# The second layer's mixture of experts: a run-time branch for each expert, and the output bias by a one-row matmul

## The chip, the core and the metric

The kernel runs on one core of one Trainium2 chip, as one launch. The metric is the device time of that core in microseconds. All data are 32-bit floats. The activations stay on the chip from the first load to the last store: `x_sb`, 128 partitions by 32 tiles of 128 columns, 4096 tokens of 128 features in all.

## The reference, cut to what matters

Six residual steps follow each other on `x` of shape (4, 1024, 128): mixture 0, a selective scan, mixture 0 again, mixture 1, attention over 16 heads and 16 "wavelengths", mixture 1 again. The change touches mixture 1 alone, which is run twice, before and after the attention:

```python
def _L1_ffn_ref(tokens, gate_w, w1, b1, w2, b2):
    ...
    cap = int(CAPACITY_FACTOR * N / E)
    x = tokens.reshape(N, H)
    probs = jax.nn.softmax(x @ gate_w.T, axis=-1)
    top2_w, top2_idx = jax.lax.top_k(probs, 2)
    ...
    counts = jnp.bincount(a_e, length=E)
    keep = counts <= cap
    valid = keep[a_e]
    ...
    h = jax.nn.silu(jnp.einsum('ech,efh->ecf', buf, w1) + b1[:, None, :])
    y = jnp.einsum('ecf,egf->ecg', h, w2) + b2[:, None, :]
    contrib = y[a_e, p] * (a_w * valid.astype(x.dtype))[:, None]
    out = contrib.reshape(N, 2, H).sum(axis=1)
    ...
x = x + 0.5 * _L1_ffn_ref(_layernorm(x, axis=-1), ...)
```

N is 4096 tokens, E is 8 experts, every token goes to its two best ones. The capacity is int(1.25 x 4096 / 8) = 640. An expert that more than 640 tokens chose is dropped as a whole: all of its contributions count as zero.

## The kernel before, in words

Everything is written with a tile framework that orders the instructions of each engine by itself and sets the semaphores. `STAGES` (line 1003) lists the stages; each group of stages loads its weights first, by DMAs on SyncE's queue (line 952), into memory that the group before has released.

`moe1` (line 388) is mixture 1. Its first half, the routing, loops over four groups of 1024 tokens. For each it takes the layer norm and transposes it into `xnt` (lines 73 to 112), forms the gate's logits on TensorE (`lg`, line 120), and ranks the experts of every token on VectorE (lines 121 to 141). This leaves `w`: for every token and expert, half the softmax weight where the expert is one of the best two, and zero elsewhere. Then the counts are summed over the tokens, across partitions by a matmul with ones (`pc`, line 416), compared with the capacity (`keep`, line 418), and `w` is multiplied by the result (line 419). So a dropped expert has weight zero for every token.

The second half computes densely: every expert runs on all tokens, whatever its weights. It loops over eight blocks of 512 tokens. In a block comes first the output bias for all experts at once: the four tiles of `w` are transposed (line 429), copied to SBUF by ScalarE (line 431), multiplied with the 8 x 128 matrix of biases (line 434) and added to `x_sb` (line 435). Then, for each of the eight experts, one unit of work: one matmul of 512 columns into `hp` (line 440), SiLU with bias on ScalarE (line 442), four matmuls of 128 columns into `op` (line 445), and four VectorE instructions that add `op` times the token's weight to `x_sb` (line 449). A matmul of 32-bit floats is two instructions with two weight loads. A call of `moe1` has 64 such units, 128 in the two calls. `hp` and `op` have three PSUM buffers each, `h` four in SBUF.

After the first call comes `attention`. It loads its own weights, works out two small tables, and has the kernel's only run-time branch: a flag is loaded into a register of every engine (line 574) and `tc.If` (line 580) chooses between two bodies. In this run the first body is executed and the second, long one is jumped over at the end. Inside, ScalarE takes 1024 exponentials of 128 x 8192 elements (line 804). After the second call of `moe1` the four quarters of `x_sb` are stored by DMAs (line 1029), each when its eight tiles are final.

Of the kernel before, what the change touches and what calls it, by code (L numbers as in the profile page):

```python
# [19 lines left out]
F32 = mybir.dt.float32  # L20
I32 = mybir.dt.int32
AF = mybir.ActivationFunctionType
ALU = mybir.AluOpType
AX = mybir.AxisListType
PSUM = bass.MemoryType.PSUM

P = 128
B, L, C = 4, 1024, 128
GT = L // P
NT = B * GT  # L30
E = 8
FS = 2
CAP = int(1.25 * B * L / E)
# [59 lines left out]
def layernorm_t(nc, k, sb, ps, g, out):  # L93

    x_g = k.x_sb[:, ts(g, GT), :]
    mv = sb.tile([P, GT, 2], F32, name="ln_mv")
    rstd = sb.tile([P, GT], F32, name="ln_rstd")
    ln_stats(nc, sb, x_g, mv, rstd)
    for i0 in range(0, GT, 4):
        pt = ps.tile([P, 4, P], F32, name="pt", tag="tr")  # L100
        for i in range(i0, i0 + 4):
            xn = sb.tile([P, C], F32, name="ln_xn", bufs=4)
            nc.vector.tensor_scalar(
                xn,
                x_g[:, i, :],
                mv[:, i, 0:1],
                rstd[:, i : i + 1],
                op0=ALU.subtract,
                op1=ALU.mult,
            )  # L110
            nc.tensor.transpose(pt[:, i - i0, :], xn, k.ident)  # L111
        nc.scalar.copy(out[:, i0 * P : (i0 + 4) * P], pt.rearrange("p a b -> p (a b)"))


def route(nc, k, sb, ps, xnt, w_router, ex, mask):


    lg = ps.tile([P, GT, E], F32, name="lg", tag="tr")
    for i in range(GT):
        nc.tensor.matmul(lg[:, i, :], xnt[:, ts(i, P)], w_router, start=True, stop=True)  # L120
    mx = sb.tile([P, GT], F32, name="rt_mx")
    nc.vector.tensor_reduce(mx, lg, AX.X, ALU.max)  # L122
    d = sb.tile([P, GT, E], F32, name="rt_d")
    nc.vector.tensor_tensor(d, lg, mx[:, :, None].to_broadcast([P, GT, E]), op=ALU.subtract)
    nc.scalar.activation(ex, d, AF.Exp)

    key = sb.tile([P, GT, E], F32, name="rt_key")
    nc.vector.tensor_scalar(key, d, LN_TINY, None, op0=ALU.max)
    other = key[:, :, None, :].to_broadcast([P, GT, E, E])
    own = key[:, :, :, None].to_broadcast([P, GT, E, E])  # L130
    eq = sb.tile([P, GT, E, E], F32, name="rt_eq")
    nc.vector.tensor_tensor(eq, other, own, op=ALU.is_equal)  # L132
    nc.vector.tensor_tensor(  # L133
        eq, eq, k.tri[:, None, :, :].to_broadcast([P, GT, E, E]), op=ALU.mult
    )
    above = sb.tile([P, GT, E, E], F32, name="rt_above")
    nc.vector.tensor_tensor(above, other, own, op=ALU.is_gt)  # L137
    nc.vector.tensor_tensor(above, above, eq, op=ALU.add)  # L138
    rank = sb.tile([P, GT, E], F32, name="rt_rank")
    nc.vector.tensor_reduce(rank, above, AX.X, ALU.add)  # L140
    nc.vector.tensor_scalar(mask, rank, 2.0, None, op0=ALU.is_lt)
# [245 lines left out]
def moe1(tc, k):  # L387


    nc = tc.nc  # L390
    with (
        tc.tile_pool(name="m1_all", bufs=1) as al,
        tc.tile_pool(name="m1", bufs=2) as sb,
        tc.tile_pool(name="m1_tr", bufs=2, space=PSUM) as ps_tr,
        tc.tile_pool(name="m1_h", bufs=3, space=PSUM) as ps_h,
        tc.tile_pool(name="m1_o", bufs=3, space=PSUM) as ps_o,
    ):
        xnt = al.tile([P, B, L], F32, name="xnt")
        mask = al.tile([P, NT, E], F32, name="mask")
        w = al.tile([P, NT, E], F32, name="w")  # L400
        for g in range(B):
            layernorm_t(nc, k, sb, ps_tr, g, xnt[:, g, :])
            ex = sb.tile([P, GT, E], F32, name="ex")
            gt = ts(g, GT)
            route(nc, k, sb, ps_tr, xnt[:, g, :], k.wr1, ex, mask[:, gt, :])
            tot = sb.tile([P, GT], F32, name="tot")
            nc.vector.tensor_reduce(tot, ex, AX.X, ALU.add)
            nc.vector.reciprocal(tot, tot)
            nc.vector.scalar_tensor_tensor(
                ex, ex, 0.5, tot[:, :, None].to_broadcast([P, GT, E]), op0=ALU.mult, op1=ALU.mult  # L410
            )
            nc.vector.tensor_tensor(w[:, gt, :], ex, mask[:, gt, :], op=ALU.mult)
        cnt = al.tile([P, E], F32, name="cnt")
        nc.vector.tensor_reduce(cnt, mask.rearrange("p t e -> p e t"), AX.X, ALU.add)
        pc = ps_tr.tile([P, E], F32, name="pc", tag="tr")
        nc.tensor.matmul(pc, k.ones, cnt, start=True, stop=True)  # L416
        keep = al.tile([P, E], F32, name="keep")
        nc.vector.tensor_scalar(keep, pc, float(CAP), None, op0=ALU.is_le)
        nc.vector.tensor_tensor(
            w, w, keep[:, None, :].to_broadcast([P, NT, E]), op=ALU.mult  # L420
        )

        for blk in range(NT // 4):
            t0 = blk * 4
            g, cols = blk // 2, ts(blk % 2, 512)

            pw = ps_tr.tile([E, 4, P], F32, name="pw", tag="tr")
            for i in range(4):
                nc.tensor.transpose(pw[:, i, :], w[:, t0 + i, :], k.ident)  # L429
            wt = sb.tile([E, 4, P], F32, name="wt")  # L430
            nc.scalar.copy(wt, pw)
            op = ps_o.tile([P, 4, C], F32, name="op")
            for i in range(4):
                nc.tensor.matmul(op[:, i, :], wt[:, i, :], k.b2_1, start=True, stop=True)  # L434
            nc.vector.tensor_tensor(
                k.x_sb[:, t0 : t0 + 4, :], k.x_sb[:, t0 : t0 + 4, :], op, op=ALU.add
            )
            for e in range(E):
                hp = ps_h.tile([P, 512], F32, name="hp")
                nc.tensor.matmul(hp, k.w1_1[:, e, :], xnt[:, g, cols], start=True, stop=True)  # L440
                h = sb.tile([P, 512], F32, name="h", bufs=4)
                nc.scalar.activation(h, hp, AF.Silu, bias=k.b1_1[:, e : e + 1])  # L442
                op = ps_o.tile([P, 4, C], F32, name="op")
                for i in range(4):
                    nc.tensor.matmul(  # L445
                        op[:, i, :], h[:, ts(i, P)], k.w2_1[:, e, :], start=True, stop=True
                    )
                for i in range(4):
                    nc.vector.scalar_tensor_tensor(  # L449
                        k.x_sb[:, t0 + i, :],  # L450
                        op[:, i, :],
                        w[:, t0 + i, e : e + 1],
                        k.x_sb[:, t0 + i, :],
                        op0=ALU.mult,
                        op1=ALU.add,
                    )

# [489 lines left out]
def getter(nc, pool, k):  # L949
    def get(name, shape, src, eng=nc.sync):  # L950
        t = pool.tile(shape, F32, name=f"c_{name}", tag=f"c_{name}")
        eng.dma_start(out=t, in_=src)
        setattr(k, name, t)

    return get
# [20 lines left out]
def load1(nc, pool, k, a):  # L976

    get = getter(nc, pool, k)
    get("wr1", [C, E], a["L1_ffn_gate_w"])
    get("w1_1", [C, E, P], a["L1_ffn_w1"])  # L980
    get("b1_1", [P, E], a["L1_ffn_b1"])
    get("w2_1", [P, E, C], a["L1_ffn_w2"])
    get("b2_1", [E, C], a["L1_ffn_b2"])


def load_attention(nc, pool, k, a):
# [16 lines left out]
STAGES = (  # L1003
    (load0, (moe0, s6, moe0)),
    (load1, (moe1,)),
    (load_attention, (attention,)),
    (load1, (moe1,)),
)

# [86 lines left out]
```

## Time and profile before

| | |
|---|---|
| median of 3 runs | 8990.91 us (8985.83 to 9001.39) |
| the profiled execution | 8990.01 us, of which the span is 8988.1 us |
| busy in it: PE, ACT, DVE, POOL | 8025.7, 7765.2, 3401.7, 609.2 us |
| granted TensorE clock, mean | 0.926 of full speed |
| instructions on TensorE | 77802 matmuls, 77802 weight loads |
| DMA, whole span | 19.43 MB, of which 10.01 MB on q8 are instructions |

How to read the lines further on. Times are microseconds unless marked ns. PE is TensorE's matmul, PEld its weight load; DVE is VectorE, ACT is ScalarE, POOL is GpSimd, SP is SyncE. A name with a q at its end (PEldq, DVEq, SPq) is the engine's sequencer, which executes waits, register loads, branches and DMA issues; these are not counted as busy. "x" is a number of instructions. A group's line ends with busy time, the mean ns of one, then the idle time of the engine just before it and who ended that. In a timeline the columns are start, length, engine, line, operation, and in brackets the idle time before. "issue" as a releaser means that the engine waited for nothing that the profile shows.

### The profile page before, as it was taken

How to read it: one execution, taken by the hardware profiler on the slowest of the kernel's cores; microseconds unless marked ns; L12 is line 12 of the kernel's file. 1: busy time of each engine (PE TensorE's matmuls, PEld its weight loads, DVE VectorE, ACT ScalarE, POOL GpSimd, SP SyncE). 2: the span in 40 equal slices, each digit the busy share in tenths (PEclk: the TensorE clock that was granted, in tenths of full speed). 3: DMA queues.
4: the chain of work that ended last, by engine and by line, in shares of the span. 5: the costliest groups of instructions: out<-in, count | busy, mean ns of one | idle time of the engine just before them, and what ended most of it. 6: DMA issues, size and time to landing. Idle time of an engine off the chain costs nothing. (4 is left out here: it accounts for less than half of the span.)

```text
span 8988.1 us, 167582 instructions
## 1 busy us (share of the span) xinstructions
PE 8025.7 (89%) x77802; PEld 3526.4 (39%) x77802; DVE 3401.7 (38%) x5903; ACT 7765.2 (86%) x1891; POOL 609.2 (7%) x579
## 2 busy tenths in 40 slices
PE   8888888899999998999999999898999998989877
PEld 5222265333333333333333333333333333333335
DVE  6776765333333333333233323333333233333225
ACT  3333333999999999999999999999999999999993
POOL 3444530000000000000000000000000000000000
PEclk9777798999999999999999999999999999999998
DMA  0000000000000000000000000000000000000000
GB/s 18 0 0 0 0 6 3 1 1 1 1 1 1 1 1 1 1 1 1 1 1 1 1 1 1 1 1 1 1 1 1 1 1 1 1 1 1 1 1 15
DMA packets 14355, 19.43 MB, mean 2 GB/s; under 512 B 3000, under 2 KB 12752, under 8 KB 13648
## 3 DMA queue, kind: packets, MB, share of 16 engines
q8 instruction: 611, 10.01, 0.5%
q1 hardware_dynamic: 9344, 6.01, 0.2%
q10 hardware_dynamic: 4304, 2.62, 0.1%
q14 instruction: 96, 0.79, 0.0%
HBM read 6.53 MB, written 2.10 MB: 1 GB/s over the span
## 5 line engine op out<-in xcount | busy, mean ns | idle before, releaser
L804 ACT ACTIVATE p_w<-xs,cc 128x8192 f32<-128x8192 f32 x1024 | 7187.6, 7109 | 37.8 <-DVE xs L742 26.8
L813 PE MATMUL o<-p_w,vt 128*9 128x256 f32 x65536 | 4051.5, 403 | 647.7 <-ACT p_w L804 645.5
L813 PEld LDWEIGHTS o<-p_w,vt 128*9 128x9 f32 x65536 | 1798.9, 95 | 2607.7 <-ACT p_w L804 799.9
L821 DVE COPY os<-o 128x256 f32<-128x256 f32 x1024 | 434.8, 425 | 3583.2 <-PE o L813 3583.0
L704 PE MATMUL s<-kp,qp 32*128 32x512 f32 x2048 | 1023.1, 619 | 0.0
L704 PE MATMUL s<-qp,kp 32*128 32x512 f32 x2048 | 1021.6, 618 | 0.0
L742 DVE COPY xs<-s 128x1024 f32<-128x1024 f32 x512 | 627.1, 1225 | 730.5 <-PE s L704 716.1
L718 DVE TENSOR_REDUCE nm<-s 128x1 f32<-128x1024 f32 x512 | 626.4, 1223 | 644.6 <-PE s L704 644.6
L704 PEld LDWEIGHTS s<-qp,kp 32*128 32x128 f32 x2048 | 343.1, 185 | 491.6 <-issue 487.4
L704 PEld LDWEIGHTS s<-kp,qp 32*128 32x128 f32 x2048 | 343.2, 186 | 470.7 <-issue 465.4
L834 PEld LDWEIGHTS pt<-ident,os 128*128 128x128 f32 x2048 | 205.7, 141 | 763.6 <-issue 667.6
L354 PE MATMUL yp<-hm,ident 128*128 128x512 f32 x512 | 382.8, 867 | 104.9 <-POOL hm L353 103.0
L834 PE MATMUL pt<-ident,os 128*128 128x128 f32 x2048 | 448.7, 301 | 20.0 <-DVE os L821 9.6
L336 ACT ACTIVATE da<-delta,neg_a 128x512 f32<-128x512 f32 x256 | 182.7, 721 | 299.0 <-DVE hst L342 298.5
L353 POOL TENSOR_TENSOR hm<-hst,c_sb 128x512 f32<-128x512 f32 x256 | 370.2, 1459 | 168.9 <-ACT c_sb L333 115.3
L178 ACT ACTIVATE r<-hp 128x512 f32<-128x512 f32 x160 | 95.6, 597 | 206.6 <-PE hp L176 185.7
L354 PEld LDWEIGHTS yp<-hm,ident 128*128 128x128 f32 x512 | 108.1, 248 | 349.7 <-POOL hm L353 317.5
L340 DVE TENSOR_TENSOR db<-du,bp 128x512 f32<-128x512 f32 x256 | 164.1, 681 | 162.9 <-PE bp L329 162.0
L442 ACT ACTIVATE h<-hp,c_b 128x512 f32<-128x512 f32 x128 | 87.6, 687 | 154.0 <-PE hp L440 153.9
L333 ACT COPY c_sb<-cp 128x512 f32<-128x512 f32 x128 | 74.9, 585 | 161.1 <-PE cp L331 126.3
L342 DVE TENSOR_TENSOR_SCAN hst<-da,last,db 128x512 f32<-128x512 f32 x128 | 190.6, 1528 | 0.0
L180 POOL TENSOR_TENSOR h<-r 128x512 f32<-128x512 f32 x160 | 164.8, 1048 | 200.7 <-ACT r L178 200.2
(180 smaller groups left out, 3820.1 us busy)
## 6 DMA issues: line engine op xcount, KB each, us to landing
x_sb<-in_L_attn_x_dram ACTq DMA_DIRECT2D x4, 512.0 KB
c_w<-in_L_ffn_w_dram SPq DMA_DIRECT2D x4, 512.0 KB
out_dram<-x_sb SPq DMA_DIRECT2D x4, 512.0 KB
c_w<-in_L_ffn_w_stack_dram SPq DMA_DIRECT2D x1, 512.0 KB
c_w<-in_L_ffn_w_stack_dram ACTq DMA_DIRECT2D x1, 512.0 KB
c_ws<-in_L_ffn_ws_dram SPq DMA_DIRECT2D x2, 128.0 KB
c_w_in<-in_L_attn_W_in_dram SPq DMA_DIRECT2D x1, 256.0 KB
c_w_out<-in_L_attn_W_out_dram SPq DMA_DIRECT2D x1, 128.0 KB
```

What stands on the lines that cost most here:

```text
L180: nc.gpsimd.tensor_tensor(h, r, r, op=ALU.mult)
L336: nc.scalar.activation(da, delta[:, c, hc], AF.Exp, scale=neg_a[:, c, n : n + 1])
L342: nc.vector.tensor_tensor_scan(hst, da, db, 0.0 if half == 0 else last[:, c, n : n + 1], op0=ALU.mult, op1=ALU.add,)
L353: nc.gpsimd.tensor_tensor(hm, hst, c_sb, op=ALU.mult)
L354: nc.tensor.matmul(yp[c], k.ident, hm, start=(n == 0), stop=(n == NS - 1))
L704: nc.tensor.matmul(s[:, ts(half, 512)], a[row, ts(i, P)], c[row, ts(half, 512)], start=True, stop=True,)
L718: nc.vector.tensor_reduce(nm[:, i : i + 1], score(j, qp[n], i, kp[n]), AX.X, ALU.max, negate=True)
L742: nc.vector.tensor_copy(xs[u][:, i, :], score(j, kp[n], i, qp[n]))
L804: nc.scalar.activation(p_w.rearrange("p a b -> p (a b)"), xs[u].rearrange("p a b -> p (a b)"), AF.Exp, scale=cc[:, h, wl : wl + 1],)
L813: nc.tensor.matmul(o[32 * r : 32 * r + D + 1, 0:QW], vts[b % 2][:, i, h, :], p_w[:, i, ts(r, QW)], start=(i == 0), stop=(i == GT - 1),)
L821: nc.vector.tensor_copy(os, o[:, 0:QW])
L834: nc.tensor.transpose(pt[:, wl % 2 * 2 + c, :], os[:, ts(c, P)], k.ident)
```

## The change

`moe1` alone is changed, and how one of its inputs is loaded.

- `keep` becomes an integer tile, and `w` is no longer multiplied by it. Two new VectorE instructions follow: `least`, the smallest of the eight counts, and `some`, whether that one is within the capacity.
- The loop over blocks and experts is turned inside out: `expert(e)` runs one expert over all eight blocks. It stands in `tc.If` on `keep[e]`, and the eight of these stand in an outer `tc.If` on `some`. `truth` loads one value into a register of every engine.
- The bias of all experts at once (transposes, copy, matmul, addition) is gone. In its place every one of the four `op` matmuls of a unit is followed by one that accumulates onto the same PSUM area: a row of ones times the expert's row of `b2`. The bias matrix is loaded as one row on one partition instead of eight rows.

```diff
-        keep = al.tile([P, E], F32, name="keep")
+        keep = al.tile([P, E], I32, name="keep")
         nc.vector.tensor_scalar(keep, pc, float(CAP), None, op0=ALU.is_le)
-        nc.vector.tensor_tensor(
-            w, w, keep[:, None, :].to_broadcast([P, NT, E]), op=ALU.mult
-        )
-
-        for blk in range(NT // 4):
-            t0 = blk * 4
-            g, cols = blk // 2, ts(blk % 2, 512)
-
-            pw = ps_tr.tile([E, 4, P], F32, name="pw", tag="tr")
-            for i in range(4):
-                nc.tensor.transpose(pw[:, i, :], w[:, t0 + i, :], k.ident)
-            wt = sb.tile([E, 4, P], F32, name="wt")
-            nc.scalar.copy(wt, pw)
-            op = ps_o.tile([P, 4, C], F32, name="op")
-            for i in range(4):
-                nc.tensor.matmul(op[:, i, :], wt[:, i, :], k.b2_1, start=True, stop=True)
-            nc.vector.tensor_tensor(
-                k.x_sb[:, t0 : t0 + 4, :], k.x_sb[:, t0 : t0 + 4, :], op, op=ALU.add
-            )
-            for e in range(E):
+        some = al.tile([P, 1], I32, name="some")
+        least = al.tile([P, 1], F32, name="least")
+        nc.vector.tensor_reduce(least, pc, AX.X, ALU.min)
+        nc.vector.tensor_scalar(some, least, float(CAP), None, op0=ALU.is_le)
+
+        def truth(tile_, j):
+            return nc.values_load(
+                tile_[0:1, j : j + 1],
+                min_val=0,
+                max_val=1,
+                skip_runtime_bounds_check_because="a comparison's result is 0 or 1",
+            )
+
+        def expert(e):
+
+            for blk in range(NT // 4):
+                t0 = blk * 4
+                g, cols = blk // 2, ts(blk % 2, 512)
                 hp = ps_h.tile([P, 512], F32, name="hp")
                 nc.tensor.matmul(hp, k.w1_1[:, e, :], xnt[:, g, cols], start=True, stop=True)
                 h = sb.tile([P, 512], F32, name="h", bufs=4)
...
                 for i in range(4):
                     nc.tensor.matmul(
-                        op[:, i, :], h[:, ts(i, P)], k.w2_1[:, e, :], start=True, stop=True
+                        op[:, i, :], h[:, ts(i, P)], k.w2_1[:, e, :], start=True, stop=False
+                    )
+                    nc.tensor.matmul(
+                        op[:, i, :], k.ones[0:1, :], k.b2_1[:, e, :], start=False, stop=True
                     )
...
+        with tc.If(truth(some, 0) > 0):
+            for e in range(E):
+                with tc.If(truth(keep, e) > 0):
+                    expert(e)
...
-    get("b2_1", [E, C], a["L1_ffn_b2"])
+    get("b2_1", [1, E, C], a["L1_ffn_b2"].rearrange("(o e) c -> o e c", o=1))
```

## The prediction, made before the changed kernel was run

> **What bounds the kernel now.** I read the busy slices of the page first, then the busy time of each engine in stretches cut at the stage borders, then single stretches by groups and in order of time.
>
> ```profile
> core 0: us, PE busy (x) PEld busy (x) DVE busy (x) ACT busy (x) POOL busy (x), PEclk, DMA share, GB/s
> 1285.20:1335.30 50.10, 29.14 (x112) 21.46 (x112) 38.14 (x194) 13.28 (x20) 0.00 (x0) 0.64 0.07 22
> 1335.30:1467.20 131.90, 129.11 (x722) 90.33 (x722) 75.54 (x266) 46.43 (x69) 0.00 (x0) 0.97 0.00 1
> 1545.80:8769.30 7223.50, 6541.14 (x72817) 2787.33 (x72816) 2226.36 (x3188) 7185.60 (x1025) 0.00 (x0) 0.95 0.01 1
> 8851.40:8983.60 132.20, 129.37 (x722) 90.42 (x722) 75.65 (x266) 46.43 (x69) 0.00 (x0) 0.97 0.05 13
> ```
>
> The third row is the attention: ACT is busy 7185.6 of 7223.5 us, so it sets 80% of the span, and the change doesn't touch it. Rows two and four are the dense halves of the two calls of moe1: 131.9 and 132.2 us, PE busy in 98% of each. Nothing of another stage runs beside them: the next stage's weights (first call) and the last store (second call) wait for their end. So whatever leaves these 264 us leaves the span. The first row is the first call's routing.
>
> What one unit of expert work costs PE, in the first call's tail:
>
> ```profile
> 1451.73 1.88 PE L440 MATMUL hp<-xnt,c_w 128*128 128x512 f32 x4
> 1453.59 2.05 PE L445 MATMUL op<-c_w,h 128*128 128x128 f32 x16
> 1455.48 1.88 PE L440 MATMUL hp<-xnt,c_w 128*128 128x512 f32 x4
> ```
>
> Two units return after 3.75 us: 1.88 us a unit at full clock, PE without gaps.
>
> **Which experts run.** The profile can't say, the weights are data. Evaluating the reference's routing on its own inputs gives, for the first call, the counts 938, 1180, 733, 853, 1478, 886, 949, 1175: all over 640, so `some` is false and everything is jumped over. For the second: 960, 1100, 798, 1345, 1107, 1539, 587, 756: expert 6 alone is kept. Nearest to the limit are 587 and 733, far enough that rounding doesn't decide.
>
> **What a branch costs.** The one branch of the kernel shows it: the sequencers' rows of the flag's load and of the comparison, then VectorE at the attention's end, where the second body is jumped over.
>
> ```profile
> L574 SPq TENSOR_LOAD <-flag x1: 466/466/466, 1472.4 to 1472.4; - x1
> L574 PEldq TENSOR_LOAD <-flag x1: 492/492/492, 1472.5 to 1472.5; - x1
> L574 DVEq TENSOR_LOAD <-flag x1: 544/544/544, 1476.9 to 1476.9; - x1
> ...
> L580 PEldq COMPARE_BRANCH  x2: 92/1920/3747, 1473.0 to 8795.0; - x2
> L580 DVEq COMPARE_BRANCH  x2: 51/53/55, 1477.5 to 8796.2; - x2
> ```
>
> ```profile
> 8796.19 0.29 DVE L510 TENSOR_TENSOR x_sb<-x_sb,c_bo 128x128 f32<-128x128 f32 x1
> 8799.11 0.49 DVE L78 BATCH_NORM_STATS2 ln_st<-x_sb 128x6 f32<-128x128 f32 x2 [2.63 <-issue]
> ```
>
> A branch that falls through costs PE 0.49 (load) + 0.09 + about 0.1 of waits = 0.7 us; VectorE, with 0.54 and the next instruction 0.2 behind, 0.8 us. A branch taken over the long body held PE 3.75 us and VectorE 2.63 us[...].
>
> [...]
>
> ```profile
> q8 instruction: 611, 10.01, 0.5%
> ```
>
> 10.01 MB in 611 packets is 16 KB each, and the 155604 TensorE records over 611 are 255 instructions. An expert's body on PE will be 8 units of 2 x (2 + 8 + 8) = 36 instructions, 288, with waits some 300[...]. On VectorE it is 32 and some waits. [...] by the rows in up to 6 x (0.7 + 3.75) = 27 us. I take 20: [...] each of the next five [...] costs 0.7 + 3.2, the mean of the two taken rows.
>
> **First call.** Counted from the end of the counting matmul `pc`, at 1335.28, to the first instruction of the attention's set-up (line 551), at 1467.97 when its weights had landed: 132.7 us. All the dense half is gone. What remains in series:
> - `keep`, `least`, `some`: three small VectorE instructions at about 0.2 (keep took 0.17, a reduce of such width 0.23) = 0.6 us. The multiplication of `w` (0.43) is gone too, within the 132.7.
> - The load and branch of `some`, 0.7; TensorE's jump over 2400 instructions, 3.75.
> - The weights' DMA, queued on SP behind SP's own branch. SP jumps over few instructions (at the attention's end SP's next instruction came 0.47 us after its branch). But the memory is released by engines that must have passed the If, and PE passes last. Bounds: SP waits for none (line 551 then starts 4.2 us after `pc`, set by VectorE's 0.6 + 0.2 + 0.8 + 2.63), or for PE. I take PE[...]: 0.6 + 0.7 + 3.75 + 0.15, and 1.9 us from the issue at 1466.07 to line 551's start = 7.1 us.
>
> Gain 132.7 - 7.1 = 125.6 us (128.5 at the other end).
>
> **Second call.** From `pc`'s end (8851.41) to the end of the span (8988.1): 136.7 us. In its place:
> - flags 0.6, outer branch falling through 0.7;
> - six skips, PE last: 20 (4 to 27; VectorE and ScalarE, with short bodies, are through before);
> - expert 6: eight units. The 8 bias instructions of a unit cost as the old bias matmul of line 434 did, 8 in 1.15 us less the 0.27 that overlap what follows, about 1.0 us with the hand-over: one row fills no fewer columns than eight. 8 x (1.88 + 1.0) = 23. PE has stood idle and starts at the low clock: in the routing after 8806 a 512-column pair took 2.05 us instead of 1.02 until about 8818, so some 10 us at half rate, 5 us lost. After the last matmul 1.2 us of VectorE. Together 29.5 (26 to 34). SiLU (0.69 a unit) and VectorE (1.13) lie beside PE;
> - expert 7's skip on VectorE, ahead of the store: 2 (0 to 4);
> - the store. Before, three of the four quarters were stored during the dense half (issues at 8883.8, 8917.9, 8950.8) and only the last one, 4.5 us with the end, stood exposed. Now every quarter is final only after the Ifs: 1.57 MB more at the 290 GB/s of the last store, 5.4 us. Sum 9.9.
>
> 62.7 us; gain 74.0.
>
> **Edits at nothing or nearly.** The framework had moved seven `hp` matmul pairs of line 440 and six SiLUs with table loads into each routing stage. They delay the logits there: VectorE waits 11 us for `lg` per call, up to 4.3 at once. Without them PE is free but colder. Between -1 and +4 us a call; I take +1.5, as the delayed logits of the first group cost about 2. The bias row as one packet instead of eight: 4 KB, landed 30 us before any use; nothing, and still nothing without cover but about 0.1 us. POOL has no work here.
>
> **The sum.** 125.6 + 74.0 + 3.0 = 202.6 us off 8990.0, the profiled execution's time: 8787.4. The median of the runs is 0.9 higher, so 8788.
>
> **Rivals.**
> - *The targets are in reach* (chance 17%): [...] six skips cost 4, not 20, and the first call's jump 1 to 2 less: 8770. For it: VectorE's first branch went on 0.2 us later, and SP's jump cost 0.47. Against: the 3.75.
> - *Every If is a meeting of engines* (15%): [...] If a skip costs 6 to 7 us instead of 3.3, seven of them add 22: 8811. Against it: at line 580 PE, SP and POOL passed the branch 4 us before VectorE did.
> - *The experts do run* (3%): this ends slower. A kept expert costs 23 + 1.2 of bare work plus its branch and refill, near 27 us, a skipped one 3.3; with 8 us around, a call breaks even with its old 132 at 27k + 3.3(8 - k) + 8 = 132, k = 4.1. From five kept experts on, each call is slower, by the 64 - 13 us of the dearer bias above all. With all eight, 216 + 8 - 132 = 92 us a call, 9175. That case is excluded by arithmetic (8192 choices, 8 x 640 = 5120 places), five to seven kept only by the counts. The branch not doing what it says belongs here too.
> - The forecast as worked out: 64%. A gain handed back in the attention (1%, no change) I see no way to, as ACT doesn't wait there: it would need a colder PE to fall behind 7.1 us per exponential.
>
> **Range and chances.** Low end: skips 4, expert 26, last skip 0, routing +4, release early: 202.6 + 16 + 3.5 + 2 + 5 + 2.9 = 232.6 off, 8758. High end: skips of 6 to 7 (+22), expert 34 (+4.5), the last skip 4, routing -1 (+5): 8822. All ends at once are unlikely: 8764 to 8815. Faster by over 0.2% (18 us, about what a measurement of this kernel can tell from no change) 96%, within it 1%, slower 3%.
>
> **What would show it.** In the first call no line of hp, h or op; the weight DMAs of the attention 5 us after `pc`. In the second, 16 `hp` matmul records (two for each of 8 units) where there were 128, PE's branches 3 to 4 us long five times over, the store's four issues within 2 us, and 9.9 us from the first to the end. Wrong if PE's branches are all at 0.1 us, if an engine sits at a semaphore behind each If, or if units run in the first call.

## The result, and the profile after

| | before | after |
|---|---|---|
| median | 8988.37 us of 4 runs (8980.74 to 9001.39) | 8830.12 us of 4 runs (8825.47 to 8833.98) |
| profiled execution, its span | 8990.01, 8988.1 us | 8833.98, 8832.1 us |
| granted TensorE clock, mean | 0.926 | 0.918 |

After over before is 0.9822, with a 95% interval of 0.9805 to 0.9839: faster by 158 us. The forecast was 8788, 42 us less, and the range ended at 8815: the direction was right, and a fifth of the expected gain is missing.

The busy time of each engine in the stretches that replace the two dense halves, in the profile after: the first call from the end of `pc` to the attention's first instruction, then the second call from `pc` to the first expert matmul, the expert that runs, and the store. The columns are those of the first fence of the prediction.

```profile
core 0: us, PE busy (x) PEld busy (x) DVE busy (x) ACT busy (x) POOL busy (x), PEclk, DMA share, GB/s
1334.40:1342.50 8.10, 0.00 (x0) 0.00 (x0) 0.40 (x4) 1.28 (x1) 0.00 (x0) 0.50 0.08 18
8742.60:8767.10 24.50, 0.00 (x1) 0.00 (x0) 0.39 (x3) 1.28 (x1) 0.00 (x0) 0.50 0.03 7
8767.10:8821.90 54.80, 52.73 (x144) 32.08 (x144) 9.01 (x32) 5.50 (x8) 0.00 (x0) 0.59 0.00 1
8821.90:8832.10 10.20, 0.00 (x0) 0.00 (x0) 0.00 (x0) 0.00 (x0) 0.00 (x0) 0.50 0.73 206
```

Where the first call had 132.7 us, 8.1 are left, and no expert runs there. In the second call one expert runs: 144 matmul records, eight units of 18. That row is the surprise: PE is busy for 52.7 of 54.8 us, 6.6 us a unit where 2.9 were expected, and the granted clock is 0.59. The dense halves had 0.97.

The sequencers' rows of the inner branch, and PE's longest wait after the attention, same kernel:

```profile
L463 PEldq COMPARE_BRANCH  x10: 82/2537/4357, 8744.3 to 8820.9; - x10
L463 DVEq COMPARE_BRANCH  x10: 47/56/63, 8744.3 to 8822.0; - x10
L463 SPq COMPARE_BRANCH  x10: 38/45/50, 8744.5 to 8748.3; - x10
```

```profile
PE hp L440 <- PEq L463: 24.5, 1, 24.5
```

The columns of the branch rows are shortest, median and longest in ns. PE waits 24.5 us for its own sequencer before expert 6. Its jumps, in order, took 3.56, 2.87, 2.98, 2.58, 2.50 and 4.36 us. On VectorE a branch's own record says less: it was 0.05 us at the attention's end in before too, and 2.63 us of idle time followed. There the distance from one branch to the next counts. It is 0.7 us with the flag's load in it, once 1.1 and once 1.7, and VectorE starts its branch for expert 6 at 8749.88, PE at 8766.90. So PE is the engine that pays for the jumps.

SP's DMA issues of the same kernel:

```profile
1339.42 0.34 SPq L960 DMA_DIRECT2D c_wq<-in_L_attn_Wq_dram  x1
...
8821.96 3.92 SPq L1037 DMA_DIRECT2D out_dram<-x_sb  x4
```

PE's outer jump in the first call begins at 1335.66 and takes 3.58 us, to 1339.24. SP, past its own branch since 1335.6, issues the first weight DMA 0.18 us later. The four stores follow each other at the end.

### The profile page after: what moved, and what is told of

It is laid out like the page before. It is cut to its first block, busy times and chain, and to the rows that moved or that the text cites. A ratio compares the mean times of both kernels' runs of the same rounds, so it can differ in the third digit from the quotient of the medians.

```text
span 8832.1 us, 164134 instructions
## 1 busy us (share of the span) xinstructions
PE 7823.0 (89%) x76474; PEld 3392.0 (38%) x76474; DVE 3262.1 (37%) x5409; ACT 7665.0 (87%) x1746; POOL 608.7 (7%) x579
## 3 DMA queue, kind: packets, MB, share of 16 engines
q8 instruction: 609, 9.98, 0.5%
## 5 line engine op out<-in xcount | busy, mean ns | idle before, releaser
L812 ACT ACTIVATE p_w<-xs,cc 128x8192 f32<-128x8192 f32 x1024 | 7188.6, 7109 | 48.5 <-DVE xs L750 29.1
L342 DVE TENSOR_TENSOR_SCAN hst<-da,db 128x512 f32<-128x512 f32 x128 | 171.1, 1372 | 5.6 <-POOL hm L353 4.4
```

The lines of the kernel that those rows point to most:

```text
L342: nc.vector.tensor_tensor_scan(hst, da, db, 0.0 if half == 0 else last[:, c, n : n + 1], op0=ALU.mult, op1=ALU.add,)
L812: nc.scalar.activation(p_w.rearrange("p a b -> p (a b)"), xs[u].rearrange("p a b -> p (a b)"), AF.Exp, scale=cc[:, h, wl : wl + 1],)
```

## The experiments

The question was first why a unit costs 6.6 us. Three theories stood: A, each change between a matmul over 128 rows and one over a single row costs PE time, and there are eight such changes a unit; B, PE starts cold after its idle jumps and stays at the low clock; C, a second matmul onto the same PSUM area has to wait for the first. A further pair stood for PE's jumps: F, a jump is dear when its target is far and has to be fetched; G, it has a fixed price.

The stage lengths, in us, each from the profiled execution. "First call" runs from `keep` to the attention's first instruction, "to hp" from the second `keep` to the first expert matmul, "expert" to VectorE's last addition, "store" runs from the last group of store issues to the end, and the last column is the whole from the second `keep` to the end.

| kernel | time | first call | to hp | expert | store | second call, to the end |
|---|---|---|---|---|---|---|
| before | 8988.37 | 132.7 | – | – | 4.5 | 136.7 |
| after | 8830.12 | 8.1 | 24.5 | 54.7 | 10.1 | 89.4 |
| no bias | 8774.84 | 8.0 | 16.1 | 18.6 | 10.1 | 44.9 |
| bias over 128 rows | 8799.12 | 7.9 | 24.2 | 26.4 | 10.1 | 60.8 |
| one bias matmul of 512 | 8795.78 | 8.1 | 16.1 | 28.8 | 10.1 | 55.1 |
| bias alone, no branches | 9584.04 | 413.7 | – | – | 4.5 | 417.4 |
| branches alone, old bias | 8796.17 | 8.2 | 32.9 | 18.7 | 10.1 | 61.7 |
| short body | 8742.63 | 7.5 | 7.1 | 17.0 | 4.5 | 28.7 |
| no outer branch | 8840.88 | 31.0 | 22.2 | 57.3 | 10.1 | 89.7 |
| bias on VectorE | 8780.44 | 7.5 | 16.5 | 17.4 | 10.1 | 44.1 |
| that, and halves | 8772.77 | 8.1 | 12.6 | 17.4 | 10.1 | 40.2 |

The kernels from "no bias" to "no outer branch" were run once each, beside runs of before at 8990.84 (the first four) and 8994.89 (the next three). Their stages tell more than their totals, since the attention, whose code is the same in all, varies by itself (see below).

**No bias.** The one-row matmul is gone.

```diff
-  op[:, i, :], h[:, ts(i, P)], k.w2_1[:, e, :], start=True, stop=False
-  )
-  nc.tensor.matmul(
-      op[:, i, :], k.ones[0:1, :], k.b2_1[:, e, :], start=False, stop=True
+  op[:, i, :], h[:, ts(i, P)], k.w2_1[:, e, :], start=True, stop=True
```

> As the changed kernel, but without the one-row bias matmuls (the output bias of mixture 1 is left out). In the changed kernel expert 6 took 54.7 us from its first hp matmul to its last VectorE addition, where 29.5 was forecast, at a granted clock of 0.59. Theory A (switching): the one-row matmul between full matmuls keeps weight loads from lying under matmuls[...]. Without it eight units run at 1.88 us after some 5 us lost to the cold start: 8 x 1.88 + 5 + 1.2 = 21 us, and the clock is full after about 10 us. Theory B (cold start): TensorE stood idle for 24 us in the skips, and the clock stays low through the whole expert whatever it does: 8 x 3.75 + 1.2 = 31 us, clock near 0.5. Theory C (accumulation): the second matmul onto the same PSUM area waits for the first: 21 us as A.

The expert took 18.6 us, 36.1 less. Its stretches by engine, up to its first matmul and from there:

```profile
core 0: us, PE busy (x) PEld busy (x) DVE busy (x) ACT busy (x) POOL busy (x), PEclk, DMA share, GB/s
8728.10:8744.30 16.20, 0.04 (x1) 0.07 (x1) 0.39 (x3) 1.28 (x1) 0.00 (x0) 0.50 0.02 7
8744.30:8762.90 18.60, 16.55 (x80) 10.61 (x80) 8.64 (x32) 5.50 (x8) 0.00 (x0) 0.91 0.01 2
```

PE starts after the same sort of idle time at clock 0.50, yet the mean over the expert is 0.91: the clock is full 3.2 us after the first matmul. So the cold start is a matter of a few us, and B falls. The stretch up to the first `hp` is shorter too, 16.1 us for 24.5; the short body takes that up.

**Bias over 128 rows.** The same number of matmuls onto the same PSUM, but the row of `b2` stands in a tile of 128 rows whose others are zero.

```diff
+  b2_full = al.tile([P, E, C], F32, name="b2_full")
+  nc.gpsimd.memset(b2_full, 0.0)
+  nc.gpsimd.tensor_copy(b2_full[0:1, :, :], k.b2_1)
...
-  op[:, i, :], k.ones[0:1, :], k.b2_1[:, e, :], start=False, stop=True
+  op[:, i, :], k.ones, b2_full[:, e, :], start=False, stop=True
```

> As the changed kernel, but the bias matmul has 128 rows: the ones matrix against the bias row padded with 127 rows of zeros. The same number of instructions, the same accumulation, columns and order; only the rows differ. Theory A: nothing is switched any more, the loads lie under the matmuls, the clock rises: 8 x 2.88 + 5 + 1.2 = 29 to 30 us, the 29.5 of the forecast. Theory B: all at half clock, but overlapped: 8 x 5.6 + 1.2 = 46 us. Theory C: unchanged, 54 to 55 us. If A is right the run is about 25 us below the changed kernel, less what the attention varies by itself.

26.4 us instead of 54.7: with 128 times as many rows the expert is 28 us shorter, which neither B nor C allows. Few rows are not dear among their like either: the 8-row matmuls of line 434 in before took 1.15 us for eight in a row. PE in order of time, in this kernel and then in after:

```profile
8768.02 0.39 PE L451 MATMUL op<-b_full,ones 128*128 128x128 f32 x2
8768.13 0.30 PEld L448 LDWEIGHTS op<-c_w,h 128*128 128x128 f32 x2
8768.24 0.39 PE L448 MATMUL op<-c_w,h 128*128 128x128 f32 x2
8768.35 0.30 PEld L451 LDWEIGHTS op<-b_full,ones 128*128 128x128 f32 x2
8768.46 0.39 PE L451 MATMUL op<-b_full,ones 128*128 128x128 f32 x2
```

```profile
8775.17 0.30 PEld L445 LDWEIGHTS op<-c_w,h 128*128 128x128 f32 x2
8775.17 0.49 PE L445 MATMUL op<-c_w,h 128*128 128x128 f32 x2
8775.59 0.29 PEld L448 LDWEIGHTS op<-c_b,ones 1*128 1x128 f32 x2
8775.59 0.48 PE L448 MATMUL op<-c_b,ones 1*128 1x128 f32 x2
8776.00 0.49 PE L445 MATMUL op<-c_w,h 128*128 128x128 f32 x2
8776.42 0.58 PE L448 MATMUL op<-c_b,ones 1*128 1x128 f32 x2
8776.93 0.80 PE L445 MATMUL op<-c_w,h 128*128 128x128 f32 x2
8777.65 0.79 PE L448 MATMUL op<-c_b,ones 1*128 1x128 f32 x2
8778.37 0.80 PE L445 MATMUL op<-c_w,h 128*128 128x128 f32 x2
```

Read the starts. With equal rows a pair follows the last after 0.22 us. Where 1 and 128 rows alternate it follows after 0.415, full-row pairs too; and at 8776.7 the clock drops, and the step becomes 0.72. A pair here is the two passes of one 32-bit product.

The weight loads show where the time goes. With equal rows the first load of a pair starts 0.11 us ahead of its matmul, under the pair before (8768.13 and 8768.24). Where rows alternate, load and matmul start together (8775.17 and 8775.17), so nothing covers the first load. One load took 0.19 us, and 0.22 + 0.19 is 0.41, the step that was seen; at half clock a load took 0.28 to 0.29, and two passes of equal rows 0.43 (in "one bias matmul of 512", before its clock rose), again the sum. That each change exposes one weight load is worked out from these rows and fits them to about 0.01 us; why the load doesn't go ahead, they don't show.

**One bias matmul of 512.** The same one-row product, but once per unit over all four blocks of columns, ahead of the four `op` matmuls: two changes a unit instead of eight.

```diff
+  nc.tensor.matmul(op, k.ones[0:1, :],
+      k.b2_1[:, e, None, :].to_broadcast([1, 4, C]), start=True, stop=False)
   for i in range(4):
-      op[:, i, :], h[:, ts(i, P)], k.w2_1[:, e, :], start=True, stop=False
...
-      op[:, i, :], k.ones[0:1, :], k.b2_1[:, e, :], start=False, stop=True
+      op[:, i, :], h[:, ts(i, P)], k.w2_1[:, e, :], start=False, stop=(i == 3)
```

> As the changed kernel, but the bias of a unit is one one-row matmul of 512 columns ahead of its four full matmuls, in place of four of 128 columns between them: two changes of the row count a unit instead of eight. Theory A: a unit costs 1.88 + 0.86 for the 512 columns + about 0.4 at the two changes = 3.1 us[...]: 8 x 3.1 + 5 + 1.2 = 31 us. Theory B: 46 us. Theory C: each full matmul accumulates onto an area long written, so near 30 us as well.

28.8 us, at a mean clock of 0.88. One unit, in order of time:

```profile
8764.45 1.02 PE L440 MATMUL hp<-xnt,c_w 128*128 128x512 f32 x2
8765.40 1.12 PE L444 MATMUL op<-c_b,ones 1*128 1x512 f32 x2
8766.45 1.16 PE L452 MATMUL op<-c_w,h 128*128 128x128 f32 x8
8767.45 1.02 PE L440 MATMUL hp<-xnt,c_w 128*128 128x512 f32 x2
```

3.00 us from `hp` to `hp`: the 1.88 of the bare unit and 1.1 for the bias. Two passes of 512 columns take 0.86 of it (`hp`'s passes follow each other after 0.43 in "no bias"), so some 0.27 is left for the two changes of a unit. The eight of after, at 0.19 each, come to 1.6 a unit at full clock; and here the clock is full from 8762.1 to the end of the expert, while in after it falls again and again. C falls here and in the run above, since both accumulate onto the same PSUM.

**Bias alone.** The kernel before, without its old bias block and with the one-row matmul after each of its `op` matmuls. Nothing is skipped, and PE never stands idle for long.

```diff
-  pw = ps_tr.tile([E, 4, P], F32, name="pw", tag="tr")
...
-  k.x_sb[:, t0 : t0 + 4, :], k.x_sb[:, t0 : t0 + 4, :], op, op=ALU.add
...
-  op[:, i, :], h[:, ts(i, P)], k.w2_1[:, e, :], start=True, stop=True
+  op[:, i, :], h[:, ts(i, P)], k.w2_1[:, e, :], start=True, stop=False
+  )
+  nc.tensor.matmul(
+      op[:, i, :], k.ones[0:1, :], k.b2_1[:, e, :], start=False, stop=True
```

> The kernel before with the bias part of the change alone: no branch, all eight experts on all tokens, block by block, weights of dropped experts zero as before, the bias by one-row matmuls between the four of a unit. TensorE never idles long here, so the cold start is out of the question. Theory A: 64 units a call at a clock that swings between half and full. In the changed kernel expert 6 needed 6.7 us a unit with its first units cold; 64 x 6.5 = 416 us a call in place of 132, less the old bias's 13: the whole kernel some 540 us slower than before, near 9530. If only the loads are exposed and the clock stays full, a unit costs 0.86 + 8 x 0.415 = 4.2 us: 269 a call, some 250 us slower in all, near 9240. Theory B: clock full, loads under matmuls, 2.88 a unit: 184 a call, 80 to 105 us slower, near 9080. Theory C: 4.2 us a unit, near 9240.

The dense half of the first call:

```profile
core 0: us, PE busy (x) PEld busy (x) DVE busy (x) ACT busy (x) POOL busy (x), PEclk, DMA share, GB/s
1354.90:1768.60 413.70, 409.85 (x1084) 255.08 (x1084) 72.49 (x259) 40.44 (x58) 0.00 (x0) 0.56 0.00 1
```

413.7 us for 64 units, 6.5 us a unit as in after, at clock 0.56, with PE busy for 99% of it (a part of the matmul records is missing). No idle PE stands at its start, so the low clock comes with the alternation and not with the jump before. This half of the change by itself makes the kernel 593 us slower than the run of before beside it.

**Branches alone.** After, with the old bias of all experts, masked by `keep`, moved inside the outer branch.

```diff
-  op[:, i, :], k.ones[0:1, :], k.b2_1[:, e, :], start=False, stop=True
...
   with tc.If(truth(some, 0) > 0):
+      biases()
       for e in range(E):
```

> The branch part of the change alone: the branches as in the changed kernel, the bias by the old way (transposed weights times the 8 x 128 matrix, for all experts at once), placed inside the outer branch ahead of the experts. The first call: as in the changed kernel, 8.1 us from keep to the first instruction of the attention's set-up. The second call: eight old bias blocks at about 1.6 us, colder 2.5, with their drain some 20 us; then skips as in the run without bias matmuls, since a body is again 160 TensorE instructions: 16 us; expert 6 in 18.6; store 10.1. From keep to the end 65 to 69 us in place of 89.4. If instead the branch itself, and not the bias, were to blame for the shortfall, 89 us would stay.

From `keep` to the end 61.7 us, 75.0 less than before. The old bias is not free any more when it stands alone, as the row of the stretch up to the first `hp` shows:

```profile
core 0: us, PE busy (x) PEld busy (x) DVE busy (x) ACT busy (x) POOL busy (x), PEclk, DMA share, GB/s
8732.50:8765.40 32.90, 22.10 (x97) 17.43 (x97) 6.32 (x12) 5.88 (x9) 0.00 (x0) 0.50 0.01 4
```

PE works on it for 22 us at half clock. Still the sum to the end is 27.7 us less than in after.

**Short body.** Each expert runs over the first two of eight blocks, so a body is 72 TensorE instructions and not 288. Three quarters of the experts' work are left out, and three of the four stores go out early, so only the jumps are compared.

```diff
-  for blk in range(NT // 4):
+  for blk in range(2):
```

> As the changed kernel, but every expert computes two of the eight blocks only (three quarters of the expert's work are left out), so that a body has about 75 instructions on TensorE in place of 300. Theory F (fetch): a taken branch costs 2.5 to 4.4 us [...], and 0.2 to 0.4 [...]. Six skips span 6 x 85 = 510 instructions[...]: from keep to the first hp matmul 1.5 + 6 x 0.6 + 2.5 x 2.7 = 12 us in place of 24.5; bodies of 180 instructions gave 16.1. Rival G (a fixed price of each If, by semaphores and loads): 24.5 stays, whatever the body's length.

7.1 us to `hp`, and PE's row of the branch:

```profile
L463 PEldq COMPARE_BRANCH  x10: 70/208/353, 8713.9 to 8735.3; - x10
```

Each of the six jumps took 0.21 to 0.35 us; the expected 12 us had two or three dear ones in them. So G falls: over a short body a jump is cheap, over a long one it costs 2.5 to 4.4. "No bias" stands between: a body of 160, and its six jumps took 0.36, 2.45, 0.22, 0.35, 2.48 and 2.66.

The DMA queues' rows bear on F. Here they are while PE is in its longest jump in after (8761.9 to 8766.3), and over five of the six jumps of the short body (8713.8 to 8717.7):

```profile
q8 instruction: 2, 0.03, 4.3%
```

```profile
q14 instruction: 1, 0.01, 0.8%
```

q8 moves instructions, in after 9.98 MB in 609 packets, 16 KB each. In after one of them starts within each of the six jumps, 0.07 to 1.0 us behind its beginning, and two in the longest. In the short body none starts within any of the six. In all the runs every jump of PE of 2.3 us and more has such a packet at its beginning or within its first 1.3 us, so for these F fits. That the packet brings the jump's target is inferred from the times alone. A few jumps of 0.2 us have one beside them too, and three of 1.6 to 1.9 us have none, so not every delay is accounted for.

**No outer branch.** All eight inner branches are met in the first call too.

```diff
-  with tc.If(truth(some, 0) > 0):
-      for e in range(E):
-          with tc.If(truth(keep, e) > 0):
-              expert(e)
+  for e in range(E):
+      with tc.If(truth(keep, e) > 0):
+          expert(e)
```

> As the changed kernel without the outer branch on the smallest count: both calls go through the eight inner branches. The first call, where nothing is kept: theory F gives eight missing jumps in place of one, 8 x 3.8 = 30 us of TensorE, which the attention's set-up must wait for if it waits for TensorE's passing (as the forecast took it): from keep to the set-up 33 us in place of 8.1. If the weights' DMA doesn't wait for TensorE, VectorE sets it: eight short jumps at about 0.7 with two misses, 12 us, and the set-up's first matmul comes at 32 us all the same. The second call gets 0.4 us shorter. The whole kernel 25 us slower than the changed one, attention aside.

31.0 us in the first call, 22.9 more. The first of PE's eight jumps took 0.36 us, and no packet on q8 starts in it; the seven others took 2.4 to 4.5. The whole is only 10.8 above the median of after: in this profile the exponentials are 20 us shorter than in that of after, for no reason that the edit gives. SP's first weight DMA:

```profile
1366.41 0.34 SPq L959 DMA_DIRECT2D c_wq<-in_L_attn_Wq_dram  x1
```

PE's last jump began at 1363.8 and took 2.42 us, to 1366.2. The DMA follows 0.2 us behind it, as in after. Counted from the end of `pc`, PE passes the last branch 23 us later than in after, and the DMA is issued 23 us later. The weights wait for PE's passing.

**Bias on VectorE.** No bias matmul; the bias row is loaded onto all partitions, and VectorE adds it times the expert's weight, 32 instructions of 128 columns per expert, while PE works.

```diff
+  for t in range(NT):
+      nc.vector.scalar_tensor_tensor(
+          k.x_sb[:, t, :], k.b2_1[:, ts(e, C)], w[:, t, e : e + 1],
+          k.x_sb[:, t, :], op0=ALU.mult, op1=ALU.add)
...
-  op[:, i, :], k.ones[0:1, :], k.b2_1[:, e, :], start=False, stop=True
...
-  get("b2_1", [1, E, C], a["L1_ffn_b2"].rearrange("(o e) c -> o e c", o=1))
+  get("b2_1", [P, E * C], a["L1_ffn_b2"].rearrange("e c -> (e c)").partition_broadcast(P))
```

> As the changed kernel, but the output bias is added by VectorE: 32 instructions an expert that add the token's weight times the bias row, from a copy of the biases on all partitions. TensorE then runs what it ran in the kernel without bias matmuls: expert 6 in 18.6 to 21 us, as 64 VectorE instructions at 0.29 are 18.6 us, half of them while TensorE is still jumping; keep to first hp 16.1. From keep to the end 45 to 48 us in place of 89.4. The time: 8830 - 42 = 8788, less what the changed kernel's profiled attention was long by: 8775 to 8788; ratio to the kernel before 0.976 to 0.978.

8780.44 us, median of 4 runs (8775.01 to 8788.21); over before 0.9768 (0.9751 to 0.9784). The stretches up to the expert and of it:

```profile
core 0: us, PE busy (x) PEld busy (x) DVE busy (x) ACT busy (x) POOL busy (x), PEclk, DMA share, GB/s
8729.10:8745.60 16.50, 0.00 (x0) 0.01 (x1) 6.10 (x25) 1.28 (x1) 0.00 (x0) 0.50 0.03 7
8745.60:8763.00 17.40, 16.10 (x80) 10.81 (x80) 11.29 (x43) 5.50 (x8) 0.00 (x0) 0.91 0.01 2
```

VectorE is past its branches long before PE, so some 21 of its 32 additions lie in PE's jumps (6.10 us of VectorE in the first row, where after had 0.39), and the rest beside PE's matmuls: the bias costs no time. The expert is as short as without a bias, or a little less. VectorE's own bodies are 64 instructions now, and three of its skips took 1.7 to 2.7 us from branch to branch; PE is still the last.

**That, and halves.** Two more flags, for experts 0 to 3 and 4 to 7, and a branch around each four, so that PE leaves experts 0 to 3 by one jump.

```diff
+  nc.vector.tensor_reduce(lower, pc.rearrange("p (a b) -> p a b", a=2), AX.X, ALU.min)
+  nc.vector.tensor_scalar(half, lower, float(CAP), None, op0=ALU.is_le)
...
-  for e in range(E):
-      with tc.If(truth(keep, e) > 0):
-          expert(e)
+  for a in range(2):
+      with tc.If(truth(half, a) > 0):
+          for e in range(4 * a, 4 * a + 4):
+              with tc.If(truth(keep, e) > 0):
+                  expert(e)
```

> As the kernel with the bias on VectorE, with one more level of branches: on the smallest count of the first four experts and of the last four. In the second call experts 0 to 3 are passed by one jump over 740 instructions, a miss of 3 to 4 us, then 4 and 5 by two: theory F gives 2.5 + 3.5 + 2 x 1.8 = 10 us to the first hp in place of 16.1, and two more small VectorE instructions (0.3). Rival G gives four Ifs in place of seven, a similar gain, so this run doesn't tell F from G. 5 us below the one before: 0.0006 of the time, inside the noise of the medians; the stage shows it.

8772.77 us, median of 4 runs (8771.3 to 8788.0); over before 0.9762 (0.9744 to 0.9779). To `hp` it took 12.6 us: the jump over four experts 3.72, then 0.08, and 1.86 and 2.47 for experts 4 and 5. That is 3.9 us less than the eight single branches, less than the expected gain; in whole times the two aren't told apart, as the ranges of their runs overlap. Both were timed beside seven runs of before, median 8992.88, and their medians are 50 and 57 us below that of after.

## Why the prediction was wrong in size, step by step

The profiled executions differ by 156.0 us, where the steps summed to 202.6; 46.6 are missing. (Two sums of the forecast are slightly off: the expert's terms, 23, 5 and 1.2, make 29.2 and not 29.5, and those of the low end 232.0 and not 232.6. Neither matters here.)

| step | forecast, us | measured, us | missing |
|---|---|---|---|
| first call, `pc` to the attention | 7.1 | 8.1 | 1.0 |
| routing, both calls, gained | 3.0 | 0.5 | 2.5 |
| flags, outer branch, six skips | 21.3 | 24.5 | 3.2 |
| expert 6 | 29.5 | 54.7 | 25.2 |
| last skip on VectorE | 2.0 | 0.1 | -1.9 |
| store | 9.9 | 10.1 | 0.2 |
| attention, from its first instruction to the second call | 0 | +17.3 | 17.3 |
| everything ahead of the first call's routing, 1.0 earlier | 0 | -1.0 | -1.0 |

**The step that failed** is "The 8 bias instructions of a unit cost as the old bias matmul of line 434 did ... about 1.0 us with the hand-over: one row fills no fewer columns than eight." In after the eight cost 36.1 us in eight units, 4.5 each (against "no bias"). The column count was rightly taken: over 128 rows the expert took 26.4 us, within the 26 to 34 of the forecast, and as one block of 512 columns the bias added 1.1 us a unit. What was wrong was the nearest row. The eight instructions of line 434 are consecutive, so PE changes from 128 to 8 rows and back once in a block; those of the change alternate with full ones and change at each. The rows for costing an instruction carry its neighbours with them, and the neighbours were what the change altered.

Of the 28.3 us between after and the bias over 128 rows, an estimate divides them. A unit at full clock would take 0.86 for its `hp` and 8 x 0.415 us, 4.2; eight of them with the forecast's 5 of cold start and 1.2 of tail 39.6. So about 13 us come from the longer step (64 changes at 0.19 make 12), and the other 15 from the clock. That share is argued from the rows; no run holds the clock fixed.

The clock itself, in four neighbouring stretches of expert 6 in after:

```profile
core 0: us, PE busy (x) PEld busy (x) DVE busy (x) ACT busy (x) POOL busy (x), PEclk, DMA share, GB/s
8773.30:8776.70 3.40, 3.40 (x18) 2.44 (x17) 0.59 (x3) 0.03 (x1) 0.00 (x0) 1.00 0.00 0
8776.70:8790.30 13.60, 13.60 (x34) 8.46 (x34) 2.79 (x11) 0.69 (x1) 0.00 (x0) 0.50 0.00 0
8790.30:8793.70 3.40, 3.40 (x17) 2.25 (x15) 0.00 (x0) 0.69 (x1) 0.00 (x0) 0.99 0.00 0
8793.70:8804.00 10.30, 10.30 (x24) 6.16 (x24) 2.25 (x8) 1.31 (x2) 0.00 (x0) 0.50 0.00 0
```

3.4 us at full clock, 10 to 14 at half, and again. PE is busy for 100% of these rows, and in "bias alone" for 99% of 414 us at clock 0.56; in "bias over 128 rows" it is busy for 24.4 of 26.4 us, 92%, at clock 0.91. So busy as the trace counts it, where a matmul's end is modelled, isn't what the clock follows. By the starts the passes are sparser where rows alternate: one follows after 0.21 us there, and after 0.11 with equal rows. That the clock goes by this was the author's estimate; no run shows what lets it fall.

**The skips** were forecast at 20 us with one cheap jump and five dear ones; in after all six were dear, 18.8 us of jumps where 5 x 3.2 = 16 had been put in. That the first would be cheap was the misjudgement (it took 0.36 us in "no outer branch", in the first call, and over the bodies of 160 in "no bias"). The price of a dear one held, 3.1 in the mean, but partly by luck: of the two figures behind the 3.2, 3.75 is a branch of PE and 2.63 idle time of VectorE. VectorE's last skip, ahead of the store, took 0.1 and not 2; a body there is 32 instructions and some waits, and over the 72 of the short body PE's jumps took 0.21 to 0.35.

**The first call** went as forecast, SP's DMA behind PE's jump included; "no outer branch" confirms that by moving PE's last jump. The early release, 4.2 us, is excluded. **The store** came out at 10.1 for 9.9. The routing gained 0.5 in two calls, inside the -1 to +4 a call that were allowed.

**The attention** is 17.3 us longer in after's profile than in before's, with no line of it changed: 2.8 in its set-up, 11.6 in the exponentials (7225.4 and 7237.0), 2.9 at its end. ACT sets the pace of the exponentials; its rows before and after:

```profile
L804 ACT ACTIVATE p_w<-xs,cc 128x8192 f32<-128x8192 f32 x1024 | 7187.6, 7109 | 37.8 <-DVE xs L742 26.8
L812 ACT ACTIVATE p_w<-xs,cc 128x8192 f32<-128x8192 f32 x1024 | 7188.6, 7109 | 48.5 <-DVE xs L750 29.1
```

The work is the same, the idle time is not: 37.8 and 48.5 us, of which the waits for PE's `o` are 10.8 and 19.0. So the forecast's reason for putting the attention at nothing, "ACT doesn't wait there", was wrong on the profile of before already. With the same attention code, the exponentials took 7213.6 to 7230.8 us in the nine kernels of the experiments; after's profile is the longest of all. A lasting loss of that size by the change is therefore unlikely, but the set-up was near 82 us in most kernels with branches and 79 in before, "bias alone" and also "short body", for which no cause was found. What part of the 17.3 belongs to the change stays open. It is the second largest term, and the forecast had given a change there 1%.

Of the rivals, targets in reach came true for short bodies only (0.21 to 0.35 us a jump); a meeting of engines at each If is excluded, since VectorE comes to expert 6 some 17 us ahead of PE. That more experts run did not happen: 16 `hp` matmul records, eight units. The price put on it was too low, however: with 6.5 us a unit a kept expert costs near 54 us, and a call breaks even at 54k + 3.3(8 - k) + 8 = 132, k = 1.9, rather than at 4.1 (worked out, not run).

## What to carry to other kernels

Cost an instruction together with its neighbours on the engine: a one-row matmul put between full ones cost 4.5 us a unit, where the same product in one piece cost 1.1 and on VectorE, which had time to spare, nothing (the expert took 17.4 us, and 18.6 without a bias). A branch that skips work cost PE 0.21 to 0.35 us over bodies of 72 instructions and 2.5 to 4.4 over bodies of 288, so nest a branch over many bodies where none is likely to run (without it the first call was 22.9 us longer), and look which engine passes last and what waits for it. When a large stage is gone, ask what it had hidden: here three quarters of the store, 5.6 us.

## What the hardware showed beyond that

- Alternating 1-row and 128-row fp32 matmuls followed each other after 0.415 us a pair at full clock and 0.72 at half in after; with 128 rows throughout, after 0.22 in "bias over 128 rows". The difference at full clock, 0.195, matches one weight load, 0.19, that starts with its matmul and not ahead of it.
- The granted clock fell to half for 10 to 14 us at a time in after, and for 24 in "bias alone" (1405.2 to 1429.0), while PE was busy without a gap, and averaged 0.56 over 414 us.
- A branch on PE took 0.07 to 0.09 us when it fell through, 0.21 to 0.35 over 72 instructions, either 0.2 to 0.36 or 2.5 to 2.7 over 160 in "no bias" (1.6 to 1.9 too in other runs), and 2.5 to 4.4 over 288 in the second call of after. One jump over four bodies of 160 took 3.72, where the four single jumps over the same bodies took 0.36, 2.65, 0.22 and 0.35 in "bias on VectorE".
- Loading a flag of `keep` from SBUF into PE's register took 0.30 us in after, 0.49 at the attention's flag before.
